# Graph layers of an eight-layer network: sums as exact counts times two float32r parts, and branches for late edges inside the layers

## The chip, the core and the metric

The kernel runs on one core of a Trainium2 chip. The metric is the device time of one execution in microseconds. The program is one launch; TensorE (PE) multiplies matrices into PSUM, VectorE (DVE), ScalarE (ACT) and GpSimd (POOL) work element by element, and DMA queues, started by SyncE (SP), ScalarE and GpSimd, move data between DRAM and SBUF.

## What is computed

A graph of N = 625 nodes and 10,000 edges is given by src, dst and edge_weight. Each node holds 512 features. Four graph layers and four others alternate, and each adds its result to x:

```
x = x + L0_gnn(norm(x))     # GCN
x = x + L0_ffn(norm(x))     # attention and a mixture of experts
x = x + L1_gnn(norm(x))     # weighted sum over edges
x = x + L1_ffn(norm(x))     # grouped mixture of experts
x = x + L2_gnn(norm(x))     # 4 experts of 2 SAGE layers each, the top 2 kept
x = x + L2_ffn(norm(x))     # LSTM over the 625 nodes, each step with one of 4 cells
x = x + L3_gnn(norm(x))     # 2 GCN layers, 512 -> 1024 -> 512
x = x + L3_ffn(norm(x))     # top-k attention
```

A GCN layer adds a loop to each node and sums over edges with the factor dis[src] * dis[dst], where dis is the root of the inverse degree (by source in L0, by target in L3):

```
norm = dis[row] * dis[col]
out = segment_sum(norm[:, None] * h[row], col, num_segments=n)
```

L0 applies it to x @ W.T + b, L3 to h @ W with b added behind; both end in relu. A SAGE layer is `aggr @ W_l + b_l + h @ W_r`, where aggr is the mean over the incoming edges.

## The kernel before

Nodes are 5 tiles of P = 125 on the partitions, features 4 chunks of 128. The graph is a matrix in SBUF, [P, NT, N] (source node by target node). `graph_and_L0_gnn` builds it from the edges by products of one-hot rows on TensorE: `count` holds how many edges there are, `weighted` the sum of their weights. Each tile of sources has a fixed number of slots for edges; edges beyond that are "late", and `tc.If(number > 0)` (L547) holds the code that would add them. Its count, `C.late`, decides a second branch in L2_gnn. In the profiled execution neither body runs.

All later sums over edges are matrix products with that matrix:

- `aggregate` (L221 to L225) gives the sum for one tile of targets: 5 matmuls, 512 wide, with a 125x125 block of the matrix as stationary operand.
- `aggregate_T` (L227 to L240) gives it feature by feature: for 4 chunks and 2 halves of the nodes 5 matmuls of some 313 columns (matmul L234), then a copy (L188 or L190), or with `inv` a multiplication by the row of factors (L240).
- `halves` (L242 to L245) splits a tensor: hi is the value rounded to float32r (ScalarE), lo the rest (VectorE). A product of the integer counts with hi and then with lo, both summed in PSUM, stands for the fp32 product. A float32r matmul is one instruction in the trace; an fp32 matmul is two.
- `linear` (L247, L251) and `linear_T` (L254, L258) multiply with weights; `copy` (L185 to L190) alternates VectorE and ScalarE; `normed` (L147, L150) normalizes x; `seen` (L131 to L145) takes its statistics; `rsqrt` (L120 to L129) is a root on ScalarE and a reciprocal on VectorE.

**L0**, behind the branch at L547, runs in this program order (L586 to L667): degrees; five transposes of xn (`turn`, L638); `source_row` (L618 to L621), which spreads the factors of the sources along a row by matmuls; `targets` (L594), which sums the counts by columns with a matmul of ones; `symmetric` (L607, L609), which builds the matrix m0 with both factors and the loops in it; `hidden` (L251 and the addition L644); between them `mean` (L600 to L603, the inverse degree for L2, written to DRAM), `target_row` and `target_col` (L625 and L631 to L633, the root of the inverse degree by target) and five more `symmetric`, whose matrix `sym` is written to DRAM for L3. Last, `layer` (L650, L651) takes `aggregate` with m0 in fp32, relu and the addition to x in one VectorE instruction, and the statistics.

**L2_gnn** (L1377 to L1512) first writes x to DRAM (L2_x), then calls `L2_layer`, which already uses count in float32r and `halves`: count is loaded and cast, xn is split, `aggregate_T` multiplies by inv, and per expert two layers follow. `icol`, the factors as a column, is fetched element by element from DRAM (L1420). At the end a branch on late edges (L1389, L1390) would reload x and repeat the whole layer in fp32. **L2_ffn** behind it copies x (L1571), writes it to DRAM (x4d), and starts with the matmuls L1607 and L1725; its loop of 625 steps runs from 1551 to 4426 us.

**L3_gnn** (L2104 to L2147) loads `sym`, normalizes, loads weights once the last tile of xn is there (`behind` in `weight`), takes `aggregate_T` in fp32, two halves j of W1 (L258), W2 (L251), and per tile `aggregate` in fp32 (L224), the bias, relu and addition (L2143), and `seen`.

A scheduler orders each engine's instructions between branches; the engines meet by semaphores. At a branch each engine that has work in its body loads the count into a register and branches by itself.

Of the kernel before, what the change touches and what calls it, by code (L numbers as in the profile page):

```python
# [30 lines left out]
KC = D // 128  # L31
# [21 lines left out]
class Ctx:  # L53


    def __init__(self, tc, ins, out, stack):
# [16 lines left out]
            k: self.dram.tile([P, NT, N], F32, name=f"graph_{k}") for k in ("weighted", "count", "sym")  # L73
        }
        self.inv = self.dram.tile([P, N], F32, name="graph_inv")
# [151 lines left out]
    def aggregate_T(self, ps, dst, m, h, inv=None):  # L227

        for f in range(KC):
            for i, (n0, w) in enumerate(HALVES if inv is None else EVEN):  # L230
                pa = ps.tile([128, 512], F32, name="pa")
                for j, part in enumerate(h):
                    for s in range(NT):
                        self.nc.tensor.matmul(pa[:, :w], part[:, s, f * 128:(f + 1) * 128], m[:, s, n0:n0 + w],  # L234
                                              start=not (s or j), stop=s == NT - 1 and j == len(h) - 1)
                if inv is None:
                    self.copy(i, dst[:, f, n0:n0 + w], pa[:, :w])
                else:
                    k = EVEN[0][1] - n0 if n0 else 0
                    self.nc.vector.tensor_tensor(dst[:, f, n0 + k:n0 + w], pa[:, k:w], inv[:, n0 + k:n0 + w], ALU.mult)  # L240

    def halves(self, hi, lo, src):  # L242

        self.nc.scalar.copy(hi, src)
        self.nc.vector.tensor_tensor(lo, src, hi, ALU.subtract)  # L245
# [150 lines left out]
def graph_and_L0_gnn(C):  # L396
# [11 lines left out]
    with ExitStack() as st:  # L408
# [83 lines left out]
        dcol, scol, tcol = T([P, NT], "dcol"), T([P, NT], "scol"), T([P, NT], "tcol")  # L492
        xn, h = T([P, NT, D], "xn"), T([P, NT, D], "h")
        w = C.weight(I["L0_gnn_WT"].rearrange("(k p) n -> p k n", p=128), KC)
# [15 lines left out]
        with ExitStack() as st2:  # L510
# [4 lines left out]
            for t in range(NT):  # L515
# [22 lines left out]
                nc.vector.reduce_sum(dcol[:, t:t + 1], count[:, t], axis=AX.X)  # L538

# [7 lines left out]
        with tc.If(number > 0):  # L547
            with ExitStack() as st2:
# [29 lines left out]
                nc.vector.reduce_sum(dcol, count, axis=AX.X)  # L578

        ps = E(tc.tile_pool(name="g_ps2", bufs=3, space=PSUM))  # L580
        drow, inv, trow, srow = (T([P, N], k) for k in ("drow", "inv", "trow", "srow"))
        sym, m0 = (T([P, NT, N], k) for k in ("sym", "m0"))
# [4 lines left out]
        def degrees():  # L587
            nc.vector.tensor_scalar_add(dcol, dcol, 1.0)
            C.rsqrt(scol, dcol, [P, NT])

# [8 lines left out]
        def mean():  # L599
            nc.vector.tensor_scalar_max(inv, drow, 1.0)  # L600
            nc.vector.reciprocal(inv, inv)
            nc.sync.dma_start(C.inv, inv)
            C.by_parts(C.graph["count"], count)  # L603

        def symmetric(m, t, sq, col, row):

            nc.vector.scalar_tensor_tensor(m[:, t], count[:, t], col[:, t:t + 1], row, op0=ALU.mult, op1=ALU.mult)  # L607
            diag = m[:, t, t * P:(t + 1) * P]
            nc.vector.scalar_tensor_tensor(diag, C.ident[:P, :P], sq[:, t:t + 1], diag, op0=ALU.mult, op1=ALU.add)  # L609


        ssq, tsq = T([P, NT], "ssq"), T([P, NT], "tsq")

        def source_row(t):
            if t == 0:
                nc.vector.tensor_mul(ssq, scol, scol)
            dg = C.small.tile([P, P], F32, name="junk")
            nc.vector.tensor_scalar(dg, C.ident[:P, :P], scol[:, t:t + 1], None, op0=ALU.mult)  # L618
            pr = ps.tile([128, 512], F32, name="pt")
            nc.tensor.matmul(pr[:P, :P], C.ones[:P, :P], dg, start=True, stop=True)  # L620
            nc.scalar.copy(srow[:, t * P:(t + 1) * P], pr[:P, :P])  # L621


        def target_row():
            nc.vector.tensor_scalar_add(drow, drow, 1.0)  # L625
            C.rsqrt(trow, drow, [P, N])

        def target_col():
            for t in range(NT):
                junk = C.small.tile([P, P], F32, name="junk")  # L630
                nc.vector.scalar_tensor_tensor(junk, C.ident[:P, :P], 1.0, trow[:, t * P:(t + 1) * P],  # L631
                                               op0=ALU.mult, op1=ALU.mult, accum_out=tcol[:, t:t + 1])
            nc.vector.tensor_mul(tsq, tcol, tcol)  # L633
# [7 lines left out]
        def hidden(t):  # L641
            ph = ps.tile([128, 512], F32, name="pt")
            C.linear(ph[:P], xT, t, w)
            nc.vector.tensor_add(h[:, t], ph[:P], bias[:P])  # L644

        C.stats = C.small.tile([P, NT, 6], F32, name="ln_st")

        def layer(t):
            po = ps.tile([128, 512], F32, name="pt")
            C.aggregate(po[:P], m0, t, h)  # L650
            nc.vector.scalar_tensor_tensor(C.x[:, t], po[:P], 0.0, C.x[:, t], op0=ALU.max, op1=ALU.add)  # L651
            nc.vector.bn_stats(C.stats[:, t], C.x[:, t])

        degrees()
        for t in range(NT):
            turn(t)
        for t in range(NT):
            source_row(t)
        for n0, w_ in HALVES:
            targets(n0, w_)  # L660
        for t in range(NT):
            symmetric(m0, t, ssq, scol, srow)
        hidden(0)
        mean()
        hidden(1)
        target_row()
        hidden(2)  # L667
        target_col()
        for t in (0, 1):
            symmetric(sym, t, tsq, tcol, trow)  # L670
        hidden(3)
        for t in range(2, NT):
            symmetric(sym, t, tsq, tcol, trow)
        C.by_parts(C.graph["sym"], sym)
        hidden(4)
        for t in range(NT):
            layer(t)

# [704 lines left out]
def L2_gnn(C):  # L1383

    nc, tc = C.nc, C.tc
    before = C.dram.tile([P, NT, D], F32, name="L2_x")
    C.by_parts(before, C.x)
    L2_layer(C, True)
    late = nc.values_load(C.late, min_val=0, max_val=EDGES, skip_runtime_bounds_check_because="a number of edges")  # L1389
    with tc.If(late > 0):  # L1390
        norm, small = C.norm, C.small
        with tc.tile_pool(name="d_small", bufs=2) as C.small:
            C.by_parts(C.x, before)
            for t in range(NT):
                C.seen(t)
            L2_layer(C, False)
            for kept, new in zip(norm, C.norm):
                nc.vector.tensor_copy(kept, new)
        C.norm, C.small = norm, small


def L2_layer(C, short):

# [3 lines left out]
    W = lambda name: I["L2_gnn_" + name]  # L1411
    with ExitStack() as st:
        E = st.enter_context
        pool = E(tc.tile_pool(name="d", bufs=1))
        inv = pool.tile([128, N], F32, name="inv")
        nc.scalar.dma_start(inv[:P], C.inv)
        nc.scalar.dma_start(inv[P:], C.inv[:128 - P])
        icol = pool.tile([P, NT], F32, name="icol")
        if short:
            nc.scalar.dma_start(icol, C.inv[0:1].rearrange("o (t p) -> (o p) t", p=P))  # L1420
            m = pool.tile([P, NT, N], F32R, name="m_count")
            with tc.tile_pool(name="d_count", bufs=1) as first:
                count = C.load_graph(first, "count")
                for t in range(NT):
                    C.copy(t, m[:, t], count[:, t])
        else:
            m = C.load_graph(pool, "count")
            for t in range(NT):
                nc.vector.tensor_mul(m[:, t], m[:, t], inv[:P])
# [4 lines left out]
        with tc.tile_pool(name="d_ps", bufs=2, space=PSUM) as ps:  # L1434
            C.feature_major(ps, xT, xn)
            gw = C.gate_w
            gb = C.row_bcast(pool, W("gate_b"), EX, "gb")
            pg = ps.tile([P, NT, EX], F32, name="pg")
            for t in range(NT):
                C.linear(pg[:, t], xT, t, gw)  # L1440
            pr = pool.tile([P, NT, 8], F32, name="probs")
# [3 lines left out]
            mx = pool.tile([P, NT], F32, name="gmax")  # L1445
            nc.vector.reduce_max(mx, p4, axis=AX.X)
            nc.vector.tensor_tensor(p4, p4, mx[:, :, None].to_broadcast([P, NT, EX]), ALU.subtract)
            nc.scalar.activation(p4, p4, AF.Exp)
            nc.vector.reduce_sum(mx, p4, axis=AX.X)
            nc.vector.reciprocal(mx, mx)  # L1450
            nc.vector.tensor_tensor(pr[:, :, :EX], p4, mx[:, :, None].to_broadcast([P, NT, EX]), ALU.mult)
            tv, tf = C.top8(pr, NT, pool)
            gate = pool.tile([P, NT, 8], F32, name="gate")
            second = pool.tile([P, NT, 8], F32, name="second")
            C.one_hot(gate, tf, 0, tv[:, :, 0:1], NT)
            C.one_hot(second, tf, 1, tv[:, :, 1:2], NT)
            nc.vector.tensor_add(gate, gate, second)
            bl = C.columns(pool, ps, W("bl").rearrange("e l (c p) -> (e l c) p", p=128), EX * 2 * KC, "bl")
            if short:
                with tc.tile_pool(name="d_parts", bufs=1) as parts:  # L1460
                    hi, lo = (parts.tile([P, NT, D], F32R, name=f"xn_{k}") for k in ("hi", "lo"))
                    for t in range(NT):
                        C.halves(hi[:, t], lo[:, t], xn[:, t])
                    C.aggregate_T(ps, aT, m, (hi, lo), inv)
            else:
                C.aggregate_T(ps, aT, m, (xn,))
# [4 lines left out]
        for e in range(EX):  # L1471
            wl, wr = (C.weight(W(n)[e, 0].rearrange("(k p) n -> p k n", p=128), KC) for n in ("Wl", "Wr"))
            hT = work.tile([128, KC, N], F32, name="hT")
            for c in range(KC):
                for n0, w in HALVES:
# [4 lines left out]
                                         bias=bl[:, e * 8 + c:e * 8 + c + 1])  # L1480

            wl, wr = (C.weight(W(n)[e, 1].rearrange("(k p) n -> p k n", p=128), KC) for n in ("Wl", "Wr"))
            b1 = C.row_bcast(work, W("bl")[e, 1], D, "bl1")
            if short:
                hw = [work.tile([P, NT, D], F32R, name=f"hw_{k}", bufs=1) for k in ("hi", "lo")]
            else:
                hw = [work.tile([P, NT, D], F32, name="hw")]
            for t in range(NT):
                po = ps_o.tile([P, D], F32, name="po")
                C.linear(po, hT, t, wl)  # L1490
                if short:
# [765 lines left out]
```

## Time and profile before

| | |
|---|---|
| runs shown | 4806.34 us median of 3 (4805.49 to 4810.65) |
| profiled execution | 4803.07 us; span of its instructions 4800.9 us |
| mean granted TensorE clock | 0.963 |
| busy: PE, DVE, ACT, POOL | 4399.4, 2717.5, 1221.1, 148.6 us |
| loop of L2_ffn, first to last step | 2874.5 us |
| L0 from the branch to the last matmul | 192 to 247 us |
| L2_gnn | 953 to 1330 us |
| L3_gnn | 4434 to 4570 us |

In the rows of the profile, `out<-in` names the tiles, `125x512 f32` their shapes (float32r tiles are shown as f32), `x50` the number of instructions; after the bar stand the busy time, the mean duration in ns, and the idle time of the engine before them with what ended it. ACTq or DVEq is the engine's sequencer, which handles branches, waits and DMA issues. A matmul's duration overlaps with that of the next, so a row of matmuls is better read by the distance of starts.

### The profile page before, as it was taken

The numbers are of one execution on the slowest core, as the hardware profiler recorded it, in microseconds if no ns is written. First come the engines' busy times: TensorE is split into PE (matmuls) and PEld (weight loads), VectorE is DVE, ScalarE is ACT, GpSimd is POOL, SyncE is SP. The second block draws the span as 40 slices with busy tenths as digits, with TensorE's granted clock in tenths as the row PEclk, the third lists the DMA queues.
The fourth block names the chain that finished last, engine by engine and source line by source line (L and its number), as shares of the span: only waits on it lengthen the run. The fifth ranks groups of instructions, "written<-read, shape, count | busy, mean of one in ns | idle before, by whom it ended". The sixth has DMA issues, their size and how long they took to land. (4 is left out here: it accounts for less than half of the span.)

```text
span 4800.9 us, 246168 instructions
## 1 busy us (share of the span) xinstructions
PE 4399.4 (92%) x103078; PEld 3323.2 (69%) x103078; DVE 2717.5 (57%) x14149; ACT 1221.1 (25%) x4803; POOL 148.6 (3%) x152
## 2 busy tenths in 40 slices
PE   8998997789989899999999999999999999998988
PEld 6656764466566777777777777777777777777555
DVE  7535015510264566666666666666666666666157
ACT  8533111211154122222222222222111111111136
POOL 0000002300000000000000000000000000000011
PEclk9997997789999999999999999999999999999988
DMA  1131974611065121222222222211000000000200
GB/s 42 52 135 43 331 250 137 219 45 63 27 223 183 39 45 40 45 43 46 45 44 45 44 44 46 44 42 33 8 7 7 7 8 7 7 8 14 69 14 12
DMA packets 485331, 307.56 MB, mean 64 GB/s; under 512 B 287742, under 2 KB 386426, under 8 KB 484243
## 3 DMA queue, kind: packets, MB, share of 16 engines
q1 hardware_dynamic: 466460, 281.05, 21.1%
q0 software_dynamic: 8800, 16.92, 1.2%
q10 hardware_dynamic: 9858, 7.20, 0.6%
q8 instruction: 80, 1.31, 0.1%
q14 instruction: 133, 1.09, 0.1%
HBM read 255.97 MB, written 49.07 MB: 64 GB/s over the span
## 5 line engine op out<-in xcount | busy, mean ns | idle before, releaser
L1944 PE MATMUL pa<-wp,left 128*23 128x256 bf16 x32080 | 1004.6, 274 | 0.3 <-PEq L1981 0.2
L1944 PEld LDWEIGHTS pa<-wp,left 128*23 128x23 bf16 x32080 | 802.0, 93 | 86.7 <-issue 1.1
L1953 PE MATMUL po<-w,left 128*1 128x128 f32 x15080 | 590.2, 272 | 5.6 <-issue 4.5
L1944 PE MATMUL pb<-wp,left 128*23 128x128 bf16 x30000 | 530.8, 219 | 0.0
L2022 ACT ACTIVATE act<-ga 128x12 f32<-128x12 f32 x625 | 132.8, 212 | 1481.6 <-DVE ga L2081 1481.6
L1944 PEld LDWEIGHTS pb<-wp,left 128*23 128x23 bf16 x30000 | 483.5, 94 | 4.5
L2075 DVE STREAM_TRANSPOSE col<-pa 128x256 f32<-128x256 f32 x625 | 281.8, 451 | 332.4 <-PE pa L1944 331.9
L1932 PE MATMUL pb<-wsel,act 128*4 128x8 f32 x5000 | 217.5, 170 | 181.4 <-DVE act L2091 161.6
L1932 PEld LDWEIGHTS pb<-wsel,act 128*4 128x4 f32 x5000 | 150.2, 83 | 332.4 <-DVE act L2091 311.7
L1953 PEld LDWEIGHTS po<-w,left 128*1 128x1 f32 x15080 | 315.0, 83 | 32.9 <-issue 16.3
L1992 PE MATMUL acc<-xslot,wslot 128*128 128x160 f32 x1250 | 336.9, 351 | 0.0
L1992 PEld LDWEIGHTS acc<-xslot,wslot 128*128 128x128 f32 x1250 | 185.8, 188 | 140.2 <-issue 140.0
L2017 ACT COPY xrow<-xlb 1x4 f32<-1x4 f32 x625 | 122.4, 196 | 541.0 <-ACTq L2015 541.0
L2083 DVE STREAM_TRANSPOSE col<-po 128x128 f32<-128x128 f32 x625 | 198.3, 317 | 92.9 <-PE po L1953 9.4
L2071 DVE COPY col<-gxb 128x16 f32 x625 | 114.5, 183 | 215.9 <-issue 215.9
L1937 PE MATMUL pb<-wsel,left 128*4 128x8 f32 x5000 | 217.6, 170 | 3.4 <-DVE left L2052 2.0
L1953 PE MATMUL po<-wo,left 128*1 128x128 f32 x5336 | 209.6, 272 | 4.7 <-issue 4.7
L2052 DVE TENSOR_TENSOR left<-th,so 128x4 f32<-128x4 f32 x625 | 104.6, 167 | 188.9 <-ACT th L2026 188.8
L2024 ACT ACTIVATE so<-go 128x4 f32<-128x4 f32 x625 | 128.2, 205 | 283.0 <-DVE go L2089 283.0
L2079 DVE STREAM_TRANSPOSE col<-pb 128x128 f32<-128x128 f32 x625 | 191.4, 306 | 0.3 <-PE pb L1944 0.2
L1937 PEld LDWEIGHTS pb<-wsel,left 128*4 128x4 f32 x5000 | 150.2, 83 | 59.8 <-DVE left L2052 5.0
L527 PE MATMUL wide<-hot_dst,hot_src 125*125 125x512 bf16 x640 | 177.8, 391 | 12.3 <-DVE hot_dst L507 12.3
(540 smaller groups left out, 6589.9 us busy)
## 6 DMA issues: line engine op xcount, KB each, us to landing
ring<-in_L_ffn_W_dram SPq DMA_DIRECT2D x80, 1024.0 KB
xslot<-xTd SPq DMA_DIRECT2D x384, 80.0 KB
wslot<-in_L_ffn_WihT_dram SPq DMA_DIRECT2D x384, 64.0 KB
gxb<-gx SPq DMA_DIRECT2D x124, 160.0 KB
w<-in_L_ffn_WihT_dram SPq DMA_DIRECT2D x16, 1024.0 KB
raw<-in_L_ffn_WhhT_dram SPq DMA_DIRECT2D x24, 512.0 KB
made<-ys SPq DMA_DIRECT2D x39, 256.0 KB
w<-in_L_gnn_Wl_dram SPq DMA_DIRECT2D x8, 1024.0 KB
```

The source lines that it names most:

```text
L527: nc.tensor.matmul(wide[i], hs[:, k], hd[:, :W0], start=first, stop=last)
L1932: pe.matmul(lg, c2[:, s:s + 1].to_broadcast([128, S]), wsel[:, 1, s], start=s == 0, stop=False)
L1937: m = pe.matmul(lg, hT[:, s:s + 1].to_broadcast([128, S]), wsel[:, 0, s], start=False, stop=s == KC - 1)
L1944: m = pe.matmul(out[32 * j:32 * j + 2 * GAP + 1], upper[:, s], wp[e][:, s, i, j, gs[0]:gs[1]].rearrange("p g n -> p (g n)"), start=k == 0, ...
L1953: m = pe.matmul(po[32 * j:32 * j + 1].rearrange("p (u r) -> p u r", r=32), left[:, s, 0:1], wo[e][:, s].rearrange("p (u j r) -> p j u r", ...
L1992: pe.matmul(later, wslot, xslot, start=False, stop=True, skip_group_check=True).then_inc(used)
L2017: act.copy(xrow[:, :S], xlb[b % DEEP][:, :, u + 1]).then_inc(sem["x"])
L2022: act.activation(act4[:, 0:3].rearrange("p g s -> p (g s)"), ga, AF.Tanh, scale=0.5).then_inc(sem["ifg"])
L2024: act.activation(so, go, AF.Sigmoid).then_inc(sem["so"])
L2075: dve.transpose(col[:, :8, :32], pa.rearrange("p (b r) -> p b r", r=32)).then_inc(sem["ta"])
L2079: dve.transpose(col[:, 8:12, :32], pb.rearrange("p (b r) -> p b r", r=32)).then_inc(sem["tb"])
L2083: dve.transpose(col[:, 12:, :32], po.rearrange("p (s r) -> p s r", r=32)).then_inc(sem["to"])
```

## The change

**L0.** `counted` holds count plus the identity (the loops) in float32r, made by `whole` as each tile's count is finished. h is scaled by the factor of its source and split in `halves` with a scale (ScalarE copies with scale, VectorE computes lo). The factor of the target is applied afterwards, as scale of a relu on ScalarE, and the addition to x is an instruction of its own. `source_row`, both `symmetric` series and the write of `sym` go. `inv` and `trow` are written to DRAM as rows, and five VectorE instructions each (`diagonal`) keep them as columns icol and tcol in SBUF. The body for late edges gets `L0_exact`, the layer in fp32, and sets `live` to 0, with which the factor `gain` becomes 0.

**L2.** The copy L2_x, the element-wise load of icol and the branch at the end go. inv is loaded on SyncE's queue behind count. A branch on late edges stands inside expert 0, behind the second of four chunks of the first layer (L1486 of the new kernel); its body, `L2_exact`, adds the fp32 layer to x and sets the gates to 0.

**L3.** It loads count and trow in place of sym, adds the loops, scales xn by tcol and splits it, and `aggregate_T` multiplies by trow on VectorE. In the second sum hw is scaled and split, and the target's factor is applied with the bias. A branch on late edges (L2183 of the new kernel) stands between the two halves j; its body is `L3_exact`.

```diff
-    def aggregate_T(self, ps, dst, m, h, inv=None):
+    def aggregate_T(self, ps, dst, m, h, inv=None, name="pa"):
...
+    def halves(self, hi, lo, src, scale=None):
...
+            self.nc.scalar.activation(hi, src, AF.Copy, scale=scale)
+            self.nc.vector.scalar_tensor_tensor(lo, src, scale, hi, op0=ALU.mult, op1=ALU.subtract)
+    def whole(self, dst, src, t, loops):
+        self.copy(t, dst, src)
+        if loops:
+            diag = slice(t * P, (t + 1) * P)
+            self.nc.vector.tensor_tensor(dst[:, diag], src[:, diag], self.ident[:P, :P], ALU.add)
+    def diagonal(self, col, row):
+        for t in range(NT):
+            junk = self.small.tile([P, P], F32, name="junk")
+            self.nc.vector.scalar_tensor_tensor(junk, self.ident[:P, :P], 1.0, row[:, t * P:(t + 1) * P],
+                                                op0=ALU.mult, op1=ALU.mult, accum_out=col[:, t:t + 1])
```

L0, behind its branch:

```diff
+        def target():
+            nc.vector.tensor_scalar_add(drow, drow, 1.0)
+            C.rsqrt(trow, drow, [P, N])
+            nc.sync.dma_start(C.rows["trow"], trow)
+            C.diagonal(C.cols["tcol"], trow)
         def hidden(t):
...
+            C.halves(parts[0][:, t], parts[1][:, t], h[:, t], scol[:, t:t + 1])
         def layer(t):
             po = ps.tile([128, 512], F32, name="pt")
-            C.aggregate(po[:P], m0, t, h)
-            nc.vector.scalar_tensor_tensor(C.x[:, t], po[:P], 0.0, C.x[:, t], op0=ALU.max, op1=ALU.add)
+            for i in range(2):
+                C.aggregate(po[:P], counted, t, parts[i], start=not i, stop=i == 1)
+            y = pool.tile([P, D], F32, name="y", bufs=2)
+            nc.scalar.activation(y, po[:P], AF.Relu, scale=gain[:, t:t + 1])
+            nc.vector.tensor_add(C.x[:, t], C.x[:, t], y)
```

L2 and L3:

```diff
-    before = C.dram.tile([P, NT, D], F32, name="L2_x")
-    C.by_parts(before, C.x)
-    L2_layer(C, True)
...
-            nc.scalar.dma_start(icol, C.inv[0:1].rearrange("o (t p) -> (o p) t", p=P))
...
+                if e == 0 and c == 1:
+                    late = late_edges(C)
+                    with tc.If(late > 0):
+                        L2_exact(C, xn, xT, aT, inv, bl, gate, ps_h)
+                        nc.vector.memset(gate, 0.0)
...
-        m = C.load_graph(pool, "sym")
+        count = C.load_graph(pool, "count")
+        trow = C.graph_row(pool, "trow")
...
-        C.aggregate_T(ps, aT, m, [xn])
+        for t in range(NT):
+            C.halves(parts[0][:, t], parts[1][:, t], xn[:, t], C.cols["tcol"][:, t:t + 1])
+        C.aggregate_T(ps, aT, m, parts, trow)
...
+            if j == 0:
+                late = late_edges(C)
+                with tc.If(late > 0):
+                    L3_exact(C, part, xn, count, trow, b1, b2, ps)
...
-            C.aggregate(po, m, t, hw)
+            for i in range(2):
+                C.aggregate(po, m, t, hw[i], start=not i, stop=i == 1)
             y = pool.tile([P, D], F32, name="y", bufs=2)
-            nc.vector.tensor_add(y, po, b2[:P])
+            nc.vector.scalar_tensor_tensor(y, po, gain[:, t:t + 1], b2[:P], op0=ALU.mult, op1=ALU.add)
```

## The prediction

> **What bounds the kernel now.** The page's first part gives TensorE 92% of the span, but most of that is the LSTM loop, which this change leaves alone; so I read the four touched stretches one by one. First the chain of waits from 4434 us to the end of the fourth graph layer (start, duration, what):
>
> ```profile
> 4435.59 12.40 DMA m_sym<-graph_sym
> ...
> 4448.08 22.93 PE pa L234 x80
> 4471.01 33.67 PE pa L258 x128
> 4504.68 34.33 PE po L251 x80
> 4539.01 21.48 PE po L224 x50
> ```
>
> A load, then TensorE without a gap: what its matmuls lose, the end gains. The 25 fp32 matmuls of the last line are 50 instructions, so one costs 21.48/25 = 0.86 us. Second, the timeline at the start of the third graph layer (start, duration, queue or engine, what, idle before):
>
> ```profile
> 955.41 0.28 ACTq L1420 DMA_DIRECT2D icol<-graph_inv  x1
> 955.73 12.93 ACTq L103 DMA_DIRECT2D gb<-in_L_gnn_gate_b_dram  x1
> 968.71 0.58 ACT L188 COPY xT<-pt 128x500 f32<-128x500 f32 x1 [13.10 <-DMA icol<-graph_inv]
> ...
> 969.34 1.10 PE L180 MATMUL pt<-ident,xn 125*128 125x125 f32 x4 [11.26 <-ACT xT L188]
> ...
> 985.45 2.72 PE L234 MATMUL pa<-m_count,xn_hi 125*128 125x314 f32 x8 [5.74 <-ACT xn_hi L244]
> ```
>
> ScalarE's queue holds the issue of gb for 12.93 us behind icol's 625 single values; its copy of xT is late by that, and TensorE idles 11.26 us. Third, the timeline behind that layer:
>
> ```profile
> 1330.05 0.59 ACT L1571 COPY x<-x 125x512 f32<-125x512 f32 x1 [7.40 <-DVEq L1390]
> ...
> 1337.44 4.37 PE L1607 MATMUL pt<-xT,wx 128*4 128x313 f32 x16 [0.86 <-DVE xT L190]
> ```
>
> VectorE's branch at L1390 holds everything for 7.40 us. Fourth, the groups of the first layer (195 to 250 us; "busy, mean ns | idle before"):
>
> ```profile
> L224 PE MATMUL pt<-h,m 125*125 125x512 f32 x50 | 21.7, 594 | 0.0
> L251 PE MATMUL pt<-w,xT 128*125 128x512 f32 x40 | 17.3, 592 | 0.0
> ...
> L607 DVE SCALAR_TENSOR_TENSOR m<-count,scol,srow 125x625 f32<-125x625 f32 x5 | 4.2, 870 | 0.9 <-ACT srow L621 0.9
> L601 DVE RECIPROCAL inv<-inv 125x625 f32<-125x625 f32 x1 | 4.1, 4066 | 0.0
> ```
>
> TensorE is the bound there too, back to back; VectorE is close behind.
>
> **The price of a float32r matmul.** The third layer has it already. Groups, 980 to 1320 us:
>
> ```profile
> L224 PE MATMUL pa<-hw_hi,m_count 125*125 125x512 f32 x100 | 34.5, 475 | 0.0
> L224 PE MATMUL pa<-hw_lo,m_count 125*125 125x512 f32 x100 | 26.5, 394 | 0.0
> ```
>
> Durations overlap, so I take starts: in steady rows one follows the other after 0.235 us, and 10 for a tile (hi and lo) take 2.35 us, 2.73 with the change from fp32 in front, against 4.3 us for 5 in fp32. For aggregate_T, ten 314-wide ones take 1.45 us (starts 990.75, 992.20, 993.65), so 80 take 11.6 against 22.93. [...]
>
> **L0.** Removed from TensorE: source_row (L620, x10, 2.57 us), and 21.75 becomes 11.75. But hi and lo of tiles 3 and 4 must be there first, and VectorE now does in this order: max, reciprocal 4.07, adds of h (0.63 to 0.69), five diagonals in 1.15, row add, second reciprocal 4.07, and five lo parts at the third layer's 0.62. Laid end to end behind the targets, lo of the last tile is ready at about 226.8 with hidden's matmuls done at 222.9 (225.4 now less 2.5). TensorE does the 13 products it can, waits, and ends 37 x 0.235 = 8.7 us later: 235.5 instead of 247.1. Against this: 0.85 at the end (Relu 0.72 on ScalarE, then an add 0.69, instead of one pass), 0.5 for a cast of the last tile ahead of the late-edge count. **L0: -10** (bounds -7, if VectorE delays the parts by 3 more, to -12, if it does not delay).
>
> **Start of L2.** icol's DMA and the write of L2_x (953.64) ahead of m_count's load go. Then the transposes run through from 955, the gate's matmuls (about 9 us at half clock) follow, m_count lands about as its bytes ask, casts (ACT 0.70, DVE 0.48 a tile) go beside them. I lay aggregate's start at 972.6 instead of 985.45; with it warmer, its end at 986 instead of 999.9. What is late next is the casts and m_count's landing. **-13.5** (-9 to -16).
>
> **Branch inside L2** (after e=0, c=1). It waits for ScalarE's last hT (0.2 + 0.52), a register load (0.45), the branch. In the trace ScalarE's branches cost 2.9 us at L547, 2.9 at L877, 0.2 at L1237, 0.4 at L1390; they skip 321, 260, 65 and 88 of its instructions. The new one skips 69, the one in L3 23: I take 0.3. One product of 0.86 us was ordered ahead of the branch; TensorE's own branch (3.3 to 4.3 us in all four) runs ahead of the array, 5.4 us at L1390; VectorE, idle under 16.8 us of matmuls, passes long before. **+1.5** (0 to +5, with 2.9 and a fall of the clock).
>
> **End of L2.** The branch at L1390 goes (7.40). Next in line is x4d, written and read back through DRAM in 5.06 us, and the loads behind it; L1607 starts at about 1328.7 on the old clock instead of 1337.44. **-8.7** (-6 to -10; the WihT loads landed by 1329, so they can bind).
>
> **Start of L3.** The count is as large as m_sym, so the load still lands at 4448; trow (0.3 MB) follows. Now VectorE adds casts, five diagonals, xn and lo parts behind it, and the first group ends at 4454.2; the rest goes at 1.45 a group, or at half that pace while the clock is 0.50: the granted clock was 0.50 from 4434 to 4450 and 0.64 from 4450 to 4452. L258 starts at 4463.6 to 4464.6 instead of 4471.01: **-6.5** (-3 to -8). W1's loads wait for the last xn and move from 4447.42 to about 4451.8; 3 MB took 10 us, so they land by 4461.9, with 1.7 us to spare.
>
> **Branch inside L3**, with the same terms: **+1.5** (0 to +6). **Second product of L3:** 11.75 against 21.48, but VectorE's tail per tile (y 0.75, x 0.75, bn_stats 0.69) nearly fills the 2.35 us; 0.9 is given back. **-8.8** (-6 to -10). The other parts (inv loaded on another queue, gating moved in the text, wx and bsel loaded later) lie beside longer matmuls: 0; if wx's issues hold ScalarE, three free PSUM buffers cover 2 us each.
>
> **Sum:** -10 - 13.5 + 1.5 - 8.7 - 6.5 + 1.5 - 8.8 = -44.5. The profiled execution took 4803.07 (span 4800.9, 2.2 around it); it becomes 4758.6. It lies 3.3 below the shown median of 4806.34, so I forecast **4761**. All the good ends add to -56 and all the bad ones to -20.
>
> **Rivals.** (1) *The branches cost their full price.* At L877 TensorE idled 3.90 us and the clock was 0.50 for the next 3 us, 0.71 for 4 more, which is some 2.5 us of work lost. Two times 6.4 instead of 1.5 adds 10: 4771. For it: all four TensorE branches took over 3 us. Against it: the sequencer ran ahead at L1390, and ScalarE's short skips were cheap. [...]
> (2) *Another wait takes the place of those removed* at the stage heads: m_count or W1 landing later, VectorE's two reciprocals. L0 -7, L2 start -9, L3 start -3 and L2 end -6 give -32 with the rest as forecast: 4774; with (1) too, 4784.
> (3) *Slower, by the LSTM.* Its TensorE code guesses the next cell and redoes work on a miss. Of its 624 gaps between steps about 570 lie under 5.5 us (median 4.45), and 54 above it, most at 6.0; the 2080 products beyond 30000 at L1944 are 52 repeats of 40. A miss costs 1.6 us, so the change is slower than before from 28 misses more (80 instead of 52); with 40 more, 4761 + 64 = 4825. For it: x reaches the loop with other roundings. Against it: two parts keep nearly the whole fp32 value, a choice of cell changes only in near ties, and those can remove misses as well; order and code of the loop are the same.
> (4) *It does not do what it says*: the products with counted cost what half an fp32 product does, 0.43 us, because they are not taken as float32r. Then L0, the start of L3 and its second product give back 10 + 6.5 + 8.8: 4786. The third layer's rows speak against it.
>
> **How the numbers follow.** Forecast 0.63 (4748 to 4770), rival 1 0.15, rival 2 0.12, rival 3 0.08, rival 4 0.02. The range **4746 to 4788** takes the forecast's good end and rivals 1, 2 and 4; beyond it lie (3) and the tails. A measurement of this kernel tells 0.2% (9.6 us), so up to 4796.7 counts as faster: all but rival 3 and 0.01 of rival 2's tail, 0.91. Rival 3 with 22 to 34 more misses is no change (0.02, with that tail 0.03); with more it is slower, 0.06.
>
> **What would show it.** L0: 50 float32r products per part, ended some 11.6 us earlier. L2: no long issue on ScalarE's queue and aggregate_T about 13 us earlier relative to the stage's start. L3: 80 products of 314 in about 12 us and 50 of 512 in 12 to 13. Gaps on TensorE at L1486 and L2183 under 1.5 us; over 4 with a clock of 0.50 behind them says rival 1. Loop from first to last step still 2874.5 us; if not, the sum is void.

## The result and the profile after

The changed kernel takes **4753.14 us**, median of 4 runs (4749.08 to 4763.55), beside 4805.91 for the kernel before in the same session (4801.35 to 4810.65): ratio 0.9893, 95% interval 0.9875 to 0.9912. Run again on another chip it took 4761.11 beside 4807.00, ratio 0.9905 (0.9888 to 0.9921). The forecast was 4761. The profiled execution took 4754.91, span 4753.1 against 4800.9: 47.8 us shorter, where the sum said 44.5.

I cut the span at the same instructions in both traces (us; each kernel has two profiled executions, and the second is in brackets). The head of L1_ffn runs from its second group of transposes of xin to its first product with ohs; a step of the LSTM is counted from ScalarE's activation of ga:

| stretch | before | after | difference | forecast |
|---|---|---|---|---|
| span's start to the transposes behind L0 | 251.37 (250.91) | 240.91 (241.34) | -10.5 | -10 |
| L2, first transpose to its first layer | 45.08 (45.38) | 27.52 (27.42) | -17.6 | -13.5 |
| L2, first layer to end, with its branch | 318.77 (318.76) | 319.49 (319.55) | +0.7 | +1.5 |
| end of L2 to its first x product | 18.49 (18.35) | 10.15 (10.10) | -8.3 | -8.7 |
| L3, start to its first layer | 36.06 (35.34) | 29.90 (28.83) | -6.2 | -6.5 |
| L3, both linear layers, with its branch | 68.00 (68.00) | 68.14 (68.13) | +0.1 | +1.5 |
| L3, second product and tail | 36.72 (37.77) | 27.09 (27.43) | -9.6 | -8.8 |
| **touched in all** | | | **-51.3** | **-44.5** |
| L0_ffn, MoE, L1 and L1_ffn | 703.73 (708.96) | 711.18 (712.05) | +7.5 | 0 |
| of it, head of L1_ffn | 25.03 (25.03) | 31.20 (31.21) | +6.2 | 0 |
| preparation of the LSTM | 213.88 (213.65) | 216.96 (217.02) | +3.1 | 0 |
| first 20 steps of the LSTM | 106.54 (107.86) | 101.73 (101.48) | -4.8 | 0 |
| its other steps | 2767.94 (2768.32) | 2767.73 (2768.97) | -0.2 | 0 |
| last step to the start of L3 | 8.99 (9.00) | 8.69 (8.69) | -0.3 | 0 |
| L3_ffn to the end | 225.38 (230.87) | 223.64 (226.63) | -1.7 | 0 |

The touched stretches gave 6.8 us more than the sum. The untouched ones, which the prediction held at zero, gave back 3.5 net, with single terms as large as an edit's. By the second pair of executions the touched ones gave 51.7, and the untouched ones 3.8 on top instead of taking any back. First, the groups of the changed kernel in the first layer (190 to 245 us; columns as in the prediction):

```profile
L283 PE MATMUL pt<-w,xT 128*125 128x512 f32 x40 | 17.3, 592 | 0.0
L225 PE MATMUL pt<-h_hi,counted 125*125 125x512 f32 x25 | 7.4, 413 | 0.0
L225 PE MATMUL pt<-h_lo,counted 125*125 125x512 f32 x25 | 6.8, 395 | 0.0
...
L640 DVE RECIPROCAL inv<-inv 125x625 f32<-125x625 f32 x1 | 4.1, 4065 | 0.0
L126 DVE RECIPROCAL trow<-rs_s 125x625 f32<-125x625 f32 x1 | 4.1, 4058 | 0.0
```

The fp32 group (50 instructions, 21.7 us) has become two of 25, which overlap and take 12.4 us from the first start to the last end (223.68 to 236.07); `w` is untouched at 17.3. VectorE's two reciprocals stood in the kernel before too, at the same price (4.1 us each); what is new on VectorE are the lo parts, and the ten `symmetric` passes are gone. Second, ScalarE and its queue at the start of L2 in the changed kernel, and TensorE over the same time (start, duration, engine, what, idle before):

```profile
950.84 0.36 ACTq L104 DMA_DIRECT2D gb<-in_L_gnn_gate_b_dram  x1
...
954.09 0.58 ACT L189 COPY xT<-pt 128x500 f32<-128x500 f32 x1
```

```profile
952.10 3.81 PE L181 MATMUL pt<-ident,xn 125*128 125x125 f32 x16 [7.57 <-issue]
955.70 3.76 PE L283 MATMUL pg<-gate_w,xT 128*125 128x4 f32 x32
959.32 0.90 PE L181 MATMUL pt<-ident,xn 125*128 125x125 f32 x4
...
965.15 1.68 PE L235 MATMUL pa<-m_count,xn_hi 125*128 125x314 f32 x5 [2.32 <-DVE m_count L191]
```

gb's issue takes 0.36 us instead of 12.93, the transposes no longer wait 11.26, and what is late now is the count matrix, by 2.32 us. Third, TensorE behind L2, and the VectorE row that its last transposes wait for:

```profile
1301.76 0.65 PE L181 MATMUL pt<-ident,x 125*128 125x125 f32 x4 [0.19 <-DVE xT L191]
1306.72 0.55 DVE L151 TENSOR_SCALAR x<-x,seenmv,seenr 125x512 f32<-125x512 f32 x1 [1.63 <-DMA x4d<-x]
1307.42 1.06 PE L181 MATMUL pt<-ident,x 125*128 125x125 f32 x4 [5.01 <-DVE near L1629]
1309.25 6.96 PE L1647 MATMUL pt<-xT,wx 128*4 128x313 f32 x16 [0.77 <-DVE xT L191]
```

As forecast, x4d is next in line: the last tile of x is normalized only when its write to x4d has landed, and the last transposes wait for that tile (5.01 us; the profile names `near`, the small instruction right behind it). But the 16 matmuls took 4.37 us before and now 6.96: they run mostly at a clock of 0.50, which rose only at 1314.51, and that gives 2.6 back. Fourth, L3: start, branch and second product.

```profile
4433.55 0.87 PE L235 MATMUL pa<-m_whole,xn_lo 125*128 125x314 f32 x5
...
4452.41 7.87 PE L290 MATMUL pa<-aT,w 128*128 128x313 f32 x29 [0.30 <-PEq L2183]
...
4504.07 1.33 PE L225 MATMUL po<-hw_lo,m_whole 125*125 125x512 f32 x5
4505.24 1.32 PE L225 MATMUL po<-hw_hi,m_whole 125*125 125x512 f32 x5
4506.39 1.31 PE L225 MATMUL po<-hw_lo,m_whole 125*125 125x512 f32 x5
```

L2183 is the new branch: TensorE idles 0.30 us at it. One tile of the second product, hi to hi, starts 2.30 us after the last (4505.24 and 4507.54), against 4.3 in fp32.

### The profile page after: what moved, and what is told of

Its sections match the earlier page's. It is cut to its first block, busy times and chain, and to the rows that moved or that the text cites. A ratio compares the mean times of both kernels' runs of the same rounds, so it can differ in the third digit from the quotient of the medians.

```text
span 4753.1 us, 246181 instructions
## 1 busy us (share of the span) xinstructions
PE 4370.0 (92%) x103068; PEld 3316.7 (70%) x103068; DVE 2715.8 (57%) x14167; ACT 1231.4 (26%) x4816; POOL 148.5 (3%) x152
```

## The experiments

My theory after the result: each touched stretch moved for the reason that the prediction names; the gains and losses elsewhere come from TensorE's clock, which follows the moment at which a burst of work begins. Rivals: they are chance of one execution; the start of L2 owes its gain to something else than icol; the branch at the end of L2 was dear because of its body and not its place; and the gain comes from the removed work, not from float32r.

### Both kernels once more

The edit is none: the changed kernel and the kernel before, each profiled a second time.

> The changed kernel once more. In its first profile the seven touched stretches gave 51.3 us, but 3.5 us came back in stretches that the change leaves alone: +6.2 us at the head of L1_ffn (from the second group of xin transposes to the product with ohs: 25.0 us before, 31.2 after, at a granted clock of 0.50 throughout), +3.1 in the LSTM's preparation, -5.0 in its first steps. Theory A: these are chance of the single execution (the phase of the clock's steps against the work, the first use of each cell's code), so this profile shows other values in some of them, within 25 to 32 us for the head of L1_ffn, while the touched stretches repeat to 0.5 us; ratio near 0.9893. Theory B: they follow from the change, by the new phase: the head of L1_ffn is 31 us again and the LSTM's values repeat to 0.5 us.

> The kernel before once more, for a second profile. Theory A: touched stretches as in the first profile to 0.5 us (start of L2 45.1 us from the first transposes to the first product with aT; end of L2 to L1607 18.5; start of L3 36.2); the head of L1_ffn anywhere in 25 to 32 us. Theory B: the head of L1_ffn 25 us again, the LSTM loop 2874.5 us to 0.5.

Measured: the brackets of the table. The touched stretches repeat within 1.1 us, and so does the head of L1_ffn, 31.21 against 25.03, with the kernel before in one session. So "chance" falls for it. The LSTM's first 20 steps repeat in the changed kernel (101.73 and 101.48, every step within 0.2 us). In the kernel before one long step moved from the 13th (12.41 us) to the 10th (10.66), while the other steps but these two agree within 2 us and the sum within 1.3. Over all traces of this study these 20 steps took 106.5 to 108.1 us in the three with the LSTM of the kernel before, 100.8 to 103.2 in ten of the other eleven, and 112.86 in one (no_branch, below). So the 4.8 us go with the kernel rather than with the execution; what makes a first step long was not tried.

What makes the head of L1_ffn longer is seen in the clock. The granted clock changes in every trace only on a grid of 3.413 us. Busy time in three of those steps from the first full one, kernel before and then the changed kernel (us and length; busy PE, PEld, DVE, ACT, POOL with instruction counts; granted clock; DMA share; GB/s):

```profile
771.86:775.27 3.41, 3.41 (x19) 3.06 (x17) 3.41 (x12) 1.89 (x4) 0.00 (x0) 0.50 1.05 383
775.27:778.69 3.42, 3.42 (x35) 3.42 (x34) 1.93 (x12) 2.12 (x5) 0.00 (x0) 1.00 1.04 389
778.69:782.09 3.40, 3.40 (x31) 3.32 (x31) 1.17 (x12) 1.81 (x3) 0.00 (x0) 1.00 1.03 369
```

```profile
764.97:768.38 3.41, 3.41 (x18) 3.03 (x17) 3.41 (x12) 2.31 (x4) 0.00 (x0) 0.50 1.05 384
768.38:771.79 3.41, 3.41 (x19) 3.41 (x19) 1.05 (x5) 1.07 (x2) 0.00 (x0) 0.50 1.05 386
771.79:775.21 3.42, 3.42 (x18) 3.42 (x19) 0.67 (x7) 1.73 (x4) 0.00 (x0) 0.50 1.03 376
```

Both are busy to the brim in the first step at half clock. Before, the clock is then 1.00 for two steps and 35 and 31 matmuls pass; after, it stays at 0.50, and 19 and 18 pass. The 29 that are missing are the 6 us. A busy array alone did not raise the clock: the changed kernel's three steps are all full (3.41, 3.41 and 3.42 us busy, at 0.50 in each). The burst's first transpose began 2.95 and 2.61 us behind a grid time in the two traces of before, and 2.42 and 2.25 in those of after. In the first trace of each kernel all 43 changes between its clock records lie on the grid, with 0.50 and 1.00 either side. Here a shift of half a microsecond decides over 6.2 us, 0.13% of the span and yet as much as an edit.

### Moving the start by 0.6 us, and warming TensorE

The first kernel copies the first transposed tile of L1_ffn twice, which moves the start of that burst (late1); the second gives TensorE something to do ahead of two heads (warm).

```diff
-            C.feature_major(ps, xT, xin, nc.scalar.copy)
+            def again(to, of, turn=iter(range(NT))):
+                for i in range(2 if next(turn) == 0 else 1):
+                    nc.scalar.copy(to, of)
+            C.feature_major(ps, xT, xin, again)
```

```diff
+            for i in range(3):
+                nc.tensor.matmul(warm[:P], C.ident[:P, :P], xin[:, 4], start=True, stop=True)
             C.feature_major(ps, xT, xin, nc.scalar.copy)
...
+        for i in range(2):
+            nc.tensor.matmul(warm[:P], C.ident[:P, :P], xn[:, 3], start=True, stop=True)
         C.aggregate_T(ps, aT, m, parts, trow)
```

> The changed kernel with one ScalarE copy more (0.58 us, the first xT copy of L1_ffn done twice), so that TensorE's third group of xin transposes starts that much later. In ten profiles the clock changes only at times a multiple of 3.413 us apart, and the head of L1_ffn (from that group to the product with ohs) took 25.0 us where the group began 2.61 to 2.95 us behind such a time, and 31.2 us where it began 2.25 to 2.44 behind it, with the clock at 0.50 throughout. Theory: the phase decides. The delay moves 2.4 to about 3.0, so the head takes 25 to 26 us, and the kernel gains some 5.5 us although it does more: ratio to the kernel before near 0.988. Rival: the head is slow for a cause of its own in the changed kernel: 31.2 us or more again, and the kernel is 0.6 us slower.

> The changed kernel with five fp32 matmuls whose results nobody reads: three in the pause of TensorE at the head of L1_ffn (they wait for the last tile of xin), two in the pause at the start of L3 (they wait for the fourth tile of xn). Theory: they fill a step of the clock's grid, so that the clock is up when the transposes and products behind them start: head of L1_ffn 25 to 27 us instead of 31.2, the 40 products of the first half of L3's aggregate_T up to 1.7 us shorter; in all 5 to 7 us less than the changed kernel, a ratio near 0.988. Rival: products of 4 columns keep the clock at 0.50 whatever comes ahead: 31 us, and the five matmuls cost up to 1 us each.

With the copy done twice the burst sat 2.81 us behind a grid time, the clock rose, and the head took 25.17 us: 6.0 won by work that does nothing. The windows of this kernel:

```profile
764.05:767.47 3.42, 3.42 (x19) 3.07 (x17) 3.42 (x13) 2.02 (x4) 0.00 (x0) 0.50 1.03 372
767.47:770.88 3.41, 3.41 (x34) 3.41 (x34) 1.82 (x14) 2.02 (x5) 0.00 (x0) 1.00 1.05 389
770.88:774.29 3.41, 3.41 (x31) 3.33 (x32) 1.22 (x12) 1.77 (x2) 0.00 (x0) 1.00 1.02 347
```

Over all traces of this study, a head that began 2.54 to 2.95 us behind a grid time took 25.0 to 25.2 us (before twice, before_no_icol and old_loads below, late1), and one at 2.25 to 2.44 took 31.2 (eight traces). So in these traces a limit lies between 2.44 and 2.54. Seven of the eight traces with the changed kernel's code up to this place fell below it, and one did not: the change moved the start close to the limit, mostly to the wrong side.

What the moment decides can be read from the first full step of the grid: transposes (125 columns each) fill 2.85 to 3.23 us of it in the five heads behind which the clock rose, and 2.56 to 2.76 us in the eight where it did not; the rest are the gate's matmuls of 4 columns. The start of L2, which has the same order of work, agrees: 3.03 to 3.41 us in the four traces where the clock rose behind that step, at most 2.83 in the ten others. That narrow matmuls count less for the clock is my reading of these rows and not shown: no run changed that alone.

In neither kernel did the whole gain: 4759.41 (0.9901, 0.9885 to 0.9918) and 4758.91 (0.9903, 0.9887 to 0.992), no different from the changed kernel. The warmed head took 22.29, with 0.84 ahead of it; but in both traces the start of L2 now lay 1.5 to 1.6 us behind a grid time and its first part took 16.2 instead of 13.05. Time won at one head moved the next on the grid. At L3 the two extra products won nothing: the product with the features took 14.11 us (14.24 and 14.15 without them), not 1.7 less, and behind that layer's branch TensorE stood idle 1.83 us more, for a reason that is not shown.

### The start of L2

Three kernels put parts of the old loading back into the changed one: icol's element-wise load on ScalarE's queue (icol_dma); the load of inv ahead of it there as well (inv_icol); and the write of L2_x ahead of both (old_loads). A fourth takes icol's load out of the kernel before, with five VectorE instructions in its place (before_no_icol).

```diff
-    icol = C.cols["icol"]
+    C.by_parts(C.dram.tile([P, NT, D], F32, name="L2_x"), C.x)            # old_loads
...
+        nc.scalar.dma_start(inv[:P], C.rows["inv"])                         # inv_icol, old_loads
+        nc.scalar.dma_start(inv[P:], C.rows["inv"][:128 - P])
...
+        nc.scalar.dma_start(icol, C.rows["inv"][0:1].rearrange("o (t p) -> (o p) t", p=P))   # all three
...
-            inv = C.graph_row(pool, "inv")                                  # inv_icol, old_loads
```

```diff
-            nc.scalar.dma_start(icol, C.inv[0:1].rearrange("o (t p) -> (o p) t", p=P))
...
+                nc.vector.scalar_tensor_tensor(junk, C.ident[:P, :P], 1.0, inv[:P, t * P:(t + 1) * P],
+                                               op0=ALU.mult, op1=ALU.mult, accum_out=icol[:, t:t + 1])
```

> The changed kernel with icol fetched element by element again, on ScalarE's queue ahead of gb, as before. The start of L2 took 45.1 us before and 27.5 after. Theory: the issue behind these single values held ScalarE, so nearly all of the 17.6 us come back: 40 to 45 us here, with an issue of gb of over 8 us. Rival: the write of L2_x, the other queue of inv and the order of the casts gave most of it: under 33 us here.

> With icol alone back on ScalarE's queue the start of L2 took 16.7 us (13.1 without, 30.3 before, each from the first transposes to the first product with count), and the issue of gb 0.99 us instead of 12.93: the single values alone don't hold the queue. Here inv is loaded by ScalarE again too, ahead of icol, as before; only the write of L2_x is still missing. Theory: it is the pile on one queue, inv's rows and then the single values, with the write of L2_x and the count beside it. If inv and icol suffice: an issue of gb of over 8 us. If the write of L2_x is needed: under 3 us.

> The kernel before, with icol taken from inv's row by five VectorE instructions in place of the load of single values; all else, the write of L2_x and inv on ScalarE's queue among it, stays. If the single values are needed for the long issue: gb's issue under 2 us, and the start of L2 between 16 and 24 us instead of 30.3 (inv may land late for the five instructions). If the other loads hold the queue by themselves: gb's issue stays over 8 us.

> The changed kernel with all three old transfers at the start of L2: x written to DRAM as L2_x ahead of the count, inv and icol on ScalarE's queue. The issue of gb took 12.93 us in the kernel before, 6.68 with inv and icol, 0.99 with icol alone, 0.36 in the changed kernel. Theory: the single values wait behind inv's rows, and these share the DMA engines with the count and, before, with L2_x (1.3 MB); each adds its share, so gb's issue is 11 to 13 us here. Rival: L2_x does not matter, what is left is ScalarE's order in the kernel before (gb issued ahead of the copies of xT): 6 to 8 us again. The start of L2 is then 16 to 20 us, less than the 30.3 before, since the copies of xT stand ahead of gb here.

gb's issue took 0.99 us behind icol alone, 6.68 with inv as well, 9.16 with L2_x, and 0.36 in the kernel before without icol. ScalarE in the kernel with the load of inv (a cast names float32r as fp32r):

```profile
955.89 0.58 ACT L189 COPY xT<-pt 128x500 f32<-128x500 f32 x1 [0.24 <-PE pt L181]
955.90 6.68 ACTq L104 DMA_DIRECT2D gb<-in_L_gnn_gate_b_dram  x1
962.62 0.62 ACT L246 CAST xn_hi<-xn 125x512 fp32r<-125x512 f32 x1 [6.15 <-issue]
```

So the theory that icol's single values alone held the queue 13 us fell: alone they hold it 1. But they are needed: with inv's load and the write of L2_x in place and no icol it is 0.36. It takes both, and in these runs the issue was the longer, the more transfers stood with the single values (0.99, 6.68, 9.16 us). And a long issue need not cost much: here the last copy of xT stands ahead of gb in ScalarE's order, and only a cast waits. First transpose to first aggregate took 16.71, 16.20 and 19.47 us in the three, against 30.34 before and 13.05 after; in the last the count matrix landed later (TensorE waited 5.58 for it). In the kernel before the copies stood behind gb, and that order was not rebuilt here, so that it is what makes the length count is read from the order and not shown. Of the 17.3 us that this part gained, all three old transfers together bring back 6.4; the other 10.9 are what the order would have to explain. The kernel before without icol settles less than it should: its short issue stands, but its five instructions waited 12.15 us for inv, and the stretch only fell to 27.97.

Most of the 3.2 to 3.7 us between 13.05 and the 16.20 and 16.71 of the first two is the clock again. The gate's 32 matmuls in the kernel with icol's load alone, beside 3.76 us above:

```profile
958.39 6.73 PE L283 MATMUL pg<-gate_w,xT 128*125 128x4 f32 x32
```

Three traces with the burst 2.66 to 3.04 us behind a grid time (the changed kernel twice, branch_end) gave 13.0 to 13.1 us for this part; seven at 0.92 to 2.32, which leave this loading as it is or add to it only icol, or inv and icol, gave 16.2 to 16.7.

### The branches

One kernel drops the late-edge code of L2 and L3, branch and body (no_branch); one puts L2's branch back behind its expert loop (branch_end); one puts it there with 113 idle instructions in its body, so that VectorE skips about 173, as at L1390 of before (branch_end_long). Both leave out the clearing of the gates, which matters only when there are late edges.

```diff
-                if e == 0 and c == 1:
-                    late = late_edges(C)
-                    with tc.If(late > 0):
-                        L2_exact(C, xn, xT, aT, inv, bl, gate, ps_h)
-                        nc.vector.memset(gate, 0.0)
...
+        late = late_edges(C)                                   # branch_end, branch_end_long
+        with tc.If(late > 0):
+            L2_exact(C, xn, xT, aT, inv, bl, gate, ps_h)
...
+            for i in range(113):                               # branch_end_long
+                nc.vector.memset(pad, float(i))
```

> The changed kernel without the branches inside L2 and L3, so without the code for late edges there. Theory: the branches cost 0.3 us of TensorE's time each (L2 from its first product with aT to its last matmul 319.5 us with, 318.8 to 319.3 without; L3 from its first product with W1 to the second sum 68.1 with, 67.6 to 68.0 without). Rival 1 of the prediction: 3 to 6 us each.

> The changed kernel with the branch of L2 at the end of the layer, where it stood before, with its new body (late edges would be added twice; there are none). Theory: VectorE's branch there holds the next layer up as before, so from L2's last matmul to L1607's first 16 to 19 us as before (18.5), not 10.1; and L2 from its first product with aT to its last matmul 318.8 to 319.2 instead of 319.5. Rival: the time was gained by the missing copy and body, and it stays under 13 us.

> The kernel with L2's branch at the end, and 113 idle VectorE instructions more in its body, so that VectorE skips as many as in the kernel before (173; late edges would be handled wrongly, as in the run with the branch at the end). There VectorE's branch took 6.0 us; with the branch at the end and the short body it took 0.55 us, and the way from L2's last matmul to L1607's first was 11.5 us instead of 18.5. Theory: the code skipped makes the price, so the branch takes 3 to 6 us and the way 14 to 18 us. Rival: the price was something else of the kernel before (what the branch waits for, the write of L2_x): 0.6 us and 11.5 us again.

Without branches L2 from its first layer takes 318.93 instead of 319.49 and L3's linear layers 67.60 instead of 68.14: **0.56 and 0.54 us is what these two branches inside a layer cost**. (Its total, 4778.62 in one run, is worse by 25: the LSTM's first 20 steps took 112.86, the first part of L2's start 16.20, the LSTM's preparation 2 and L3_ffn 4 more. None of that stands at a branch, and long first steps are seen in before too. L2 with its branch at the end took 318.93 and 318.94 from its first layer, as without branches.)

At the end of L2 I expected the old price from the place. It did not come: the stretch took 11.47, 1.3 more than after, not the 6 to 9 of the theory. VectorE's branch before, then in this kernel, then with the long body (kind, count, shortest, median and longest duration in ns, first and last start; the second row is the first thing behind the branch):

```profile
L1390 DVEq COMPARE_BRANCH  x1: 63/63/63, 1323.9 to 1323.9; - x1
L1390 DVEq EVENT_SEMAPHORE  x1: 21/21/21, 1329.9 to 1329.9; - x1
```

```profile
L1508 DVEq COMPARE_BRANCH  x1: 63/63/63, 1302.7 to 1302.7; - x1
L1508 DVEq EVENT_SEMAPHORE  x1: 21/21/21, 1303.2 to 1303.2; - x1
```

```profile
L1508 DVEq COMPARE_BRANCH  x1: 63/63/63, 1306.7 to 1306.7; - x1
L1508 DVEq EVENT_SEMAPHORE  x1: 21/21/21, 1309.7 to 1309.7; - x1
```

6.0, 0.5 and 3.0 us, and the stretch 18.49, 11.47 and 13.91. The longer skip made the branch dearer (3.0 against 0.5 us), as the rival has it, though the stretch stayed just short of the 14 to 18 us expected; and at about as many skipped instructions as before the branch is half as dear, so the count alone does not set it. The same branch in L1_ffn, with the same body, cost VectorE 3.43 us at L1237 of before and 0.54 at L1274 of after: so something other than the body counts too, and one skip cost 0.5 or 3.4. What that is, and what made it 6.0 us at L1390 (5.98 in the second trace), is not shown.

### The same factors in fp32

The changed kernel with counts, loops and scaled h, xn and hw kept in fp32, one part instead of two, in L0 and L3.

```diff
-    counted = T([P, NT, N], "counted", F32R)
...
-    parts = [T([P, NT, D], k, F32R) for k in ("h_hi", "h_lo")]
+    counted = T([P, NT, N], "counted")
...
+    scaled = T([P, NT, D], "h_scaled")
...
-            for i in range(2):
-                C.aggregate(po[:P], counted, t, parts[i], start=not i, stop=i == 1)
+            C.aggregate(po[:P], counted, t, scaled)
```

> The changed kernel with the sums of L0 and L3 in fp32: counted and the scaled values are kept in fp32, one part each. Theory: the matmuls' time alone comes back: L0 from its first product with counted to the next layer's transposes 25 to 26 us instead of 17.2, L3's product with the features 22.5 to 23 instead of 14.2, L3's second sum 21.5 instead of 12.3; the start of L3 is 1 to 2 us earlier without the lo parts. Together 25 to 27 us. Rival: the parts' extra work on VectorE cancels a third of it, so that the start of L3 and the end of L0 are 5 us or more better than in the changed kernel.

4788.91 us, and its three products are back at the old price: 26.46 us in L0, 23.13 for L3's first and 21.62 for its second, against 17.23, 14.24 and 12.28. So float32r gives 9.2, 8.9 and 9.3, together 27.4. That is 9.2 of L0's 10.5. In L3's start it is more than the net gain of 6.2, because some 2 are paid ahead of the first product: 13.29 and 12.82 us from the layer's first transpose to it in the two traces of before, 15.66 and 14.68 in those of after. I had put this down to the split of xn and expected 1 to 2 us back without it; but this kernel, which scales xn there without splitting it, took 14.88. In it as in the changed kernel VectorE stands idle until the count has landed (1.26 and 2.07 us), and then its casts and loops take 1.2 us ahead of the product; `m_sym` needed neither. Its groups in the first layer:

```profile
L225 PE MATMUL pt<-h_scaled,counted 125*125 125x512 f32 x50 | 21.6, 592 | 0.0
L283 PE MATMUL pt<-w,xT 128*125 128x512 f32 x40 | 17.3, 592 | 0.0
```

## Why the prediction was right

- **Float32r at 0.235 us a matmul:** held. The 50 of L3's second product took 12.28, that is 0.245 each with the change from fp32. Rival 4 fell.
- **L0, -10:** -10.5. VectorE's chain ended as worked out: lo of the last tile was there at 226.91, forecast 226.8. The wait of TensorE for it did not come, for TensorE began its transposes 1.0 us later than before (197.34, 196.34) and its first product with counted at 223.68, where hidden's matmuls were forecast done at 222.9; the last product ended at 236.07, forecast 235.5, and the stretch behind it grew by 0.6 instead of 1.35.
- **Start of L2, -13.5:** -17.6, the term that was mis-sized most. I took about 9 us at half clock for the gate's matmuls; they took 5.6 (3.76 and 1.84), since the clock rose at 956.11. In the seven traces that began earlier on the grid the gain against the first trace of before is 13.4 to 15.0, close to the forecast's, so the 4 us beyond it are luck of the grid. The reason given was half of it: icol's single values held the issue only together with the transfers ahead of them.
- **Branches, +1.5 each:** about +0.5 each against no branch (the stretches moved by +0.7 and +0.1); TensorE ran ahead as forecast, and its gaps were 0.30. Rival 1 fell.
- **End of L2, -8.7:** -8.3, with x4d next in line as named. Not forecast: 2.6 lost behind it, because the products began at half clock.
- **Start of L3, -6.5 and second product, -8.8:** -6.2 and -9.6. VectorE's tail, about 2.3 us a tile, stands close beside TensorE's 2.3, as worked out; the 0.9 set aside for it were not needed, since the stretch behind the last product got 0.3 shorter.
- **Rival 2** fell: its waits exist (2.32 for the count, 7.40 at L3's `m_whole`), but all lay inside the terms. **Rival 3** fell: 54 long gaps between steps before and 54 after.
- **"Loop still 2874.5 us; if not, the sum is void":** it was 2869.5, and the sum was not void, since nearly all of the difference (4.8 of 5.0) is in the first 20 steps. The test was too sharp: it should have left out the loop's start, which the prediction held at zero because the change leaves its code alone, and whose first 20 steps were 3 to 6 us shorter than before in ten of the eleven traces of the changed code.

So the sum was right to 3.3 us in this pair of executions, but by two errors that nearly cancel: 6.8 too little in the touched stretches, of which 4 are the clock at L2 and 2 the branches, and 3.5 lost in stretches that I held at zero. In the second pair the span fell by 55.5 us. The medians of the same changed code in two sessions, 4753.14 and 4761.11, lie 8 us apart, so that the second equals the forecast is luck; the gain, 46 and 53 us by the medians, is not.

## What to carry to other kernels

Where TensorE runs back to back, a product that takes about half the pitch, as here (0.245 us an instruction in L3's second product, against 21.48/50 = 0.43), is worth its instructions times what the pitch falls by (9.2, 8.9 and 9.3 us in the three), once the engine that prepares its parts has been laid end to end beside it. A DMA whose issue is held seems to cost what stands behind it in its engine's order (read from the rows here, not shown by a run of its own), so look at the order before the length of the issue. Edits that moved a burst of TensorE work after a pause cost or gained 3 to 6 us here by the clock's grid alone, far from the edit (6.2 at L1_ffn, 3.1 at L2): keep that much apart in the sum, and judge an edit by its own stretch in more than one trace.

## What the hardware showed beyond that

- The clock's grid of 3.413 us has one position in an execution and another in the next: its first point lay 0.04 to 3.33 us behind the span's start. Still, the phase of L1_ffn's head repeats within 0.35 us for the same code ahead of it.
- TensorE at work did not always keep its clock: in before, L1_ffn's head fell back to 0.50 at 782.09, though the step ahead of it was busy for 3.40 of 3.40 us, nearly all of it with matmuls of 4 and 32 columns.
- A queue's issue of one small DMA took 0.36, 0.99, 6.68, 9.16 and 12.93 us, by what lay ahead of it: the three long ones, 6.68 and more, stood behind both a load of single values and other transfers.
- In the first trace of each kernel a branch not taken into its body cost VectorE 0.5 to 6.0 us, ScalarE 0.2 to 3.0, and TensorE 3.3 to 4.5 us; of the last nearly all was hidden by its sequencer's lead at the two new branches, with 0.30 us of idle array at L2183.
